# Attention: one value bank copied by ScalarE and one by VectorE, and the last step's output pieces in its first eight turns

## The chip, the core and the metric

The kernel runs on one core of a Trainium2 chip. The metric is the device time of one execution in microseconds; the time before is the median of three runs. One more execution was recorded by the hardware profiler, and all durations of single instructions come from it.

## What is computed

64 sequences of 32 tokens with 512 features go through four residual layers, all in fp32. The change touches the third, an attention over a paged cache followed by a small expert layer:

```python
q = einsum('bsd,ed->bse', x, Wq).reshape(B, S, HQ, D)      # 32 heads of 128
k, v = (einsum('bsd,ed->bse', x, W).reshape(B, S, HK, D) for W in (Wk, Wv))   # 8 heads
q, k = rope(rmsnorm(q)), rope(rmsnorm(k))
k_all = concat([k_cache[block_table], k], axis=1)          # 512 cached keys + 32 own
v_all = concat([v_cache[block_table], v], axis=1)
scores = where(valid, einsum('bqhd,bkhd->bhqk', q, repeat(k_all, 4)) * SCALE, -1e30)
o = einsum('bhqk,bkhd->bqhd', softmax(scores), repeat(v_all, 4))
return einsum('bse,de->bsd', o.reshape(B, S, HQ * D), Wo)
```

## The kernel before

Layers 0 and 1 come first and are not touched. In the attention (`attention`) the 2048 tokens are 16 tiles of 128 rows, four sequences each, and the heads are done in two halves of four key heads and sixteen query heads. That gives 32 *steps*, one for each half and tile, numbered 0 to 31. A step has 16 *turns*: four sequences (`b`) by four key heads (`g`). A turn `i` on TensorE is

- `turned(i)`: four transposes of the probabilities `pr` into a PSUM tile `prT_ps`, which ScalarE copies to `prT` (L790);
- `start(i + 2)`: the scores `sc` of the turn two ahead (L772), then on VectorE the masked minimum (L777), on ScalarE the exponential (L779), on VectorE the reciprocal and the scaling (L781, L784);
- `values`: the products of cached values `vt` and `prT` into `po` (L621).

Between these, work is placed by hand in `slots`: slot `2t` runs in turn `t` between the transposes and the scores, slot `2t + 1` between the scores and the values. The slots of a step hold the projections of the next step (pv, pk, pq), which the last step does not have; the eight pieces of the output projection of the previous step (`Output.product`, two products `py` each, from turn 9 on); the loads; and in the last step four small products `pw` that prepare the next layer (`tail.fold`, turns 10 to 13).

Two sequences make a *pair*. The values of a pair accumulate in two PSUM banks `pos[0]` and `pos[1]`, two heads each. At the end of a pair, in turns 7 and 15, `own_part` adds the products with the tokens' own values and copies both banks to `oT` (L820, VectorE). The next pair's first values product writes `pos[0]` again, so it waits for that copy. `oT` of a step is what the output pieces of the next step read: pieces 0 to 3 read the rows of `pos[0]`, pieces 4 to 7 those of `pos[1]`.

The keys of a sequence are 16 loads on SyncE's queue (`load_keys`, L98), with the page numbers read into SyncE's registers ahead of them (L93). There are two key buffers: the loads of sequence `b + 2` are placed in turn 1 of sequence `b`, and start when the last scores of `b` have been computed, in that same turn. They are needed two turns ahead of the sequence. GpSimd gathers the values (L643), SyncE also loads the earlier half's output `y_before` with piece 0 and stores the finished tile `y` (L755), which VectorE makes in L751. `y` and `y_before` have one buffer each.

After step 31 its own output pieces run in one go, and then the last layer (`tail.run`). The PE order is the program's order: every TensorE instruction of the attention is chained to the one before (`on_pe`).

Of the kernel before, what the change touches and what calls it, by code (L numbers as in the profile page):

```python
# [572 lines left out]
def attention(c, known, x_in, y_part, y_out, tail):  # L573
# [10 lines left out]
    tc, nc, a = c.tc, c.nc, c.a  # L584
    half = HD // 2
    n_c = L // P
    with ExitStack() as outer:
# [31 lines left out]
        def part(out, pairs, first, last):  # L619
            for i, (lhsT, rhs) in enumerate(pairs):  # L620
                c.on_pe(nc.tensor.matmul(out, lhsT, rhs, start=first and i == 0,  # L621
                                         stop=last and i == len(pairs) - 1))
# [56 lines left out]
        class Projection:  # L679
# [43 lines left out]
            def turned(self, what):  # L723
                r = self.r.pop(what)
                pt = transposes("tq", "qkT_ps", [r[:, m, :] for m in range(REP)])
                if what == "k":
                    nc.scalar.copy(self.kT, pt)
                else:
                    nc.scalar.copy(self.qT[:, what].rearrange("p j h s -> p h j s"),
                                   pt.rearrange("p h (j s) -> p h j s", j=SEQ))  # L730
# [62 lines left out]
        def own_turned(b):  # L793
            pt = transposes("tq", "own_prT_ps", [own_prs[b % 2]])
            own_prT = wk.tile([P, P], F32, name="own_prT", bufs=2)
            nc.scalar.copy(own_prT, pt[:, 0, :])
            return own_prT
# [3 lines left out]
        def values(b, g, prT):  # L801


            if b % 2 == 0 and g == 0:
                pos[:] = [ps.tile([P, 2, 2, P], F32, tag=f"po{n}", name="po") for n in range(2)]
            part(pos[g // 2][:, b % 2, g % 2, :], [(vts[b % 2][:, n, g * HD:(g + 1) * HD], prT[:, n, :])
                                                   for n in range(n_c)], b % 2 == 0 and g % 2 == 0, False)

        def own_part(b, own_prTs, oT):


            for u in range(2):
                for g in range(2):
                    for n in range(2):
                        q = slice(n * P // 2, (n + 1) * P // 2)
                        part(pos[n][:, u, g, :], [(own_vts[u][q, g, :], own_prTs[u][q, :])],
                             False, u == g == 1)
            at = (b - 1) % SEQ * S
            for n in range(2):
                nc.vector.tensor_copy(  # L820
                    oT[:, 2 * n * REP:2 * (n + 1) * REP, at:at + 2 * S]
                    .rearrange("p m (u s) -> p m u s", u=2),
                    pos[n].rearrange("p u g (h s) -> p (g h) u s", h=REP))
# [15 lines left out]
        steps = [(h, T) for h in range(HALVES) for T in range(NT)]  # L839
# [4 lines left out]
        def of(i):  # L844
            s, j, g = turns[i]
            h, T = steps[s]
            return s, h, SEQ * T + j, g
# [3 lines left out]
        def keys_of(i):  # L851
            if i < len(turns):
                s, h, b, _ = of(i)
                new_keys(h, b)
                own_keys(h, b, projections[s].kT)
                load_keys(h, b)

        def values_of(i):
            if i < len(turns):
                s, h, b, _ = of(i)  # L860
                load_values(h, b)

        def own_values_of(i):
            if i < len(turns):
                s, _, b, _ = of(i)
                own_values(b, projections[s].v)

        def start(i):
            if i < len(turns):
                s, h, b, g = of(i)  # L870
                scores(i, projections[s], h, b, g)
# [39 lines left out]
        for s, (h, T) in enumerate(steps):  # L911
            if s:
                oTs[s] = qp.tile([P, HQP, P], F32, name="oT")
            slots = [[] for _ in range(2 * per)]
            if s == 0:
                slots[0].append(partial(projections[0].turned, 2))
                slots[2].append(partial(projections[0].turned, 3))
                slots[2].append(partial(own_keys, 0, 1, projections[0].kT))
            if s + 1 < len(steps):
                p = projections[s + 1]  # L920
                for what, at in zip(("v", "k") + GROUPS,
                                    ((1, 2), (3, 4), (6, 7), (8, 10), (11, 13), (14, 16))):
                    for u in range(2):
                        slots[at[u]].append(partial(p.product, what, u))
                for what, at in zip(("k",) + GROUPS, (9, 12, 15, 17, 20)):
                    slots[at].append(partial(p.turned, what))
            else:
                slots[16].append(tail.scaled)
                for m, at in enumerate((20, 22, 24, 26)):
                    slots[at].append(partial(tail.fold, ps, m))  # L930
            if s + 2 < len(steps):
                slots[18].append(projections[s + 2].load)
                slots[24].append(projections[s + 2].tables)
                slots[28].append(projections[s + 2].x)
                if steps[s + 2][0] != h:

                    for what, at in zip(("v", "k") + GROUPS, (3, 5, 8, 11, 14, 17)):
                        slots[at].append(partial(weights, steps[s + 2][0], what))
            if s + 2 == len(steps):
                for at, f in zip((17, 20, 23, 26, 29), tail.weights(wp, wvk)):  # L940
                    slots[at].append(f)
            if s:
                out = Output(*steps[s - 1], oTs.pop(s - 1), ws)
                for u, at in enumerate((18, 19, 21, 23, 25, 27, 29, 31)):
                    slots[at].append(partial(out.product, u))
                if steps[s - 1][0] != h:
                    for u, at in enumerate((20, 24, 28, 31)):
                        slots[at].append(partial(output_weights, h, u))
                if s > 1:
                    slots[2].append(stores.pop(0))  # L950
                stores.append(out.store)
            for t in range(per):
                i = s * per + t
                _, _, b, g = of(i)
                prT = turned(i)
                if g == HKP - 1:
                    own_prTs = ([] if b % 2 == 0 else own_prTs) + [own_turned(b)]
                for f in slots[2 * t]:
                    f()
                start(i + 2)  # L960
                if g == 1:

                    keys_of(i - 1 + 2 * HKP)
                for f in slots[2 * t + 1]:
                    f()
                values(b, g, prT)
                if b % 2 and g == HKP - 1:
                    own_part(b, own_prTs, oTs[s])
                elif b % 2 == 0 and g in (0, 2) and i >= HKP:
                    own_values_of(i - g + g // 2 * HKP)  # L970
                if g == HKP - 1:
                    values_of(i - g + 2 * HKP)
# [222 lines left out]
def emit(tc, a, layers=(0, 1, 2)):  # L1195
    with ExitStack() as ctx:
        c = Common(ctx, tc, a)
        dram = ctx.enter_context(tc.tile_pool(name="scratch", bufs=1, space=DRAM))

        def scratch(name):  # L1200
            tiles = [dram.tile([P, D], F32, name=f"{name}_{t}") for t in range(NT)]
            return lambda t: tiles[t]

        def rows(name):
            return lambda t: a[name][t * P:(t + 1) * P, :]

        x = rows("x")
        for n in layers:
            out = rows("out") if n == layers[-1] else scratch(f"x{n}")
            if n == 0:  # L1210
                layer0(c, x, out)
            if n != 0 and n == next(m for m in layers if m):
                kp = ctx.enter_context(tc.tile_pool(name="known", bufs=1))
                last = Tail(c)
                last.numbers(kp)
                known = Known(c, kp)
            if n == 1:
                layer1(c, kp, x, out)
            elif n == 2:
                y_part, y = scratch("y_part"), scratch("y")  # L1220
                attention(c, known, x, y_part, y, last.between(x, y, out))
            x = out
# [86 lines left out]
```

## Time and profile before

| | us |
|---|---|
| median of three timed runs | 3705.31 (3702.78 to 3708.0) |
| the profiled execution | 3732.76 |
| its span, first to last instruction | 3730.8 |
| TensorE busy in the span | 3643.1 (98%) |
| VectorE, ScalarE, GpSimd busy | 1807.6, 1277.1, 1261.9 |

Times in the profile count from the start of the span. The attention's turns run from about 1100 to 3544 us, its last step from 3465.86, the last layer from 3560. PE is TensorE, PEld its weight loads, DVE VectorE, ACT ScalarE, POOL GpSimd, and SPq the queue of SyncE. In a row such as `3470.86 1.55 PE L621 MATMUL ... x8 [3.43 <-ACT prT L790]` the numbers are the start, the duration of the merged group, and in brackets how long the engine was idle before it and what ended that. In the chain the durations are issue times, without the overlapped tail of a product. Matmul counts are twice those of the source, [...]. PEclk is the granted share of the TensorE clock.

### The profile page before, as it was taken

How to read it: one execution, taken by the hardware profiler on the slowest of the kernel's cores; microseconds unless marked ns; L12 is line 12 of the kernel's file. 1: busy time of each engine (PE TensorE's matmuls, PEld its weight loads, DVE VectorE, ACT ScalarE, POOL GpSimd, SP SyncE). 2: the span in 40 equal slices, each digit the busy share in tenths (PEclk: the TensorE clock that was granted, in tenths of full speed). 3: DMA queues.
4: the chain of work that ended last, by engine and by line, in shares of the span. 5: the costliest groups of instructions: out<-in, count | busy, mean ns of one | idle time of the engine just before them, and what ended most of it. 6: DMA issues, size and time to landing. Idle time of an engine off the chain costs nothing.

```text
span 3730.8 us, 62064 instructions
## 1 busy us (share of the span) xinstructions
PE 3643.1 (98%) x18752; PEld 2526.2 (68%) x18752; DVE 1807.6 (48%) x4879; ACT 1277.1 (34%) x2950; POOL 1261.9 (34%) x1265
## 2 busy tenths in 40 slices
PE   6999999999999999999999999999999999999899
PEld 3444788888866777677667766677766776677655
DVE  5443222222236555565556555565556655565333
ACT  0111111211124444444444444444444444444311
POOL 0112100000035444544444444444445444444222
PEclk9999999999999999999999999999999999999999
DMA  5104211111044444334443356444444344434321
GB/s 195 34 24 162 99 43 60 43 49 36 32 145 129 123 119 124 115 116 119 121 118 114 117 177 188 153 125 122 122 127 122 118 123 123 123 117 143 119 71 60
DMA packets 408827, 407.68 MB, mean 109 GB/s; under 512 B 49232, under 2 KB 321616, under 8 KB 408496
## 3 DMA queue, kind: packets, MB, share of 16 engines
q1 hardware_dynamic: 361776, 251.65, 22.1%
q0 software_dynamic: 44416, 147.88, 12.8%
q10 hardware_dynamic: 2304, 4.20, 0.3%
q8 instruction: 152, 2.49, 0.3%
q14 instruction: 179, 1.47, 0.1%
HBM read 382.57 MB, written 20.97 MB: 108 GB/s over the span
## 4 chain that ended last, share of the span: by engine, by line
PE 93%; SPq 2%; issue 1%; DVE 1%; another core or an unknown queue 1%; DMA 1%; DVEq 1%; ACT 1%; POOL 0%; ACTq 0%; POOLq 0%
PE po L621 14%; PE sc L772 12%; PE pq L621 11%; PE py L621 11%; PE gate_up L292 10%; PE prT_ps L616 6%; PE pz L292 5%; PE po L1079 3%; PE pk L621 3%; PE ph L122 3%; PE pv L621 3%; PE pd L228 2%; PE po L292 2%; PE qkT_ps L616 2%; PE py L183 1%
## 5 line engine op out<-in xcount | busy, mean ns | idle before, releaser
L643 POOL DMA_INDIRECT vt<-in_v_rows,v_rows x512 | 500.7, 978 | 805.6 <-PE po L621 693.2
L621 PEld LDWEIGHTS po<-prT,vt 128*128 128x128 f32 x4096 | 530.6, 192 | 212.2 <-issue 185.1
L777 DVE CUSTOM_DVE_ANT_0 pr<-sc,mask 128x544 f32<-128x544 f32 x512 | 368.7, 720 | 477.7 <-PE sc L772 394.0
L772 PE MATMUL sc<-kt,qT 128*128 128x288 f32 (+1 forms) x2048 | 557.6, 395 | 12.2 <-DMA kt<-in_kT 8.0
L621 PE MATMUL po<-prT,vt 128*128 128x128 f32 x4096 | 545.3, 276 | 22.1 <-ACT prT L790 18.5
L779 ACT ACTIVATE pr<-pr,low 128x544 f32<-128x544 f32 x512 | 383.6, 749 | 486.7 <-DVE low L777 484.4
L772 PEld LDWEIGHTS sc<-kt,qT 128*128 128x128 f32 x2048 | 369.8, 191 | 189.9 <-issue 83.9
L621 PE MATMUL py<-wo,oT 128*128 128x512 f32 x1024 | 480.5, 593 | 0.8 <-DVE oT L820 0.8
L621 PE MATMUL pq<-wq,xT 128*128 128x512 f32 x1024 | 480.8, 593 | 0.0
L790 ACT COPY prT<-prT_ps 128x512 f32<-128x512 f32 x512 | 298.6, 583 | 441.2 <-PE prT_ps L616 279.6
L784 DVE TENSOR_SCALAR pr<-pr,low 128x512 f32<-128x512 f32 x512 | 324.1, 633 | 16.8
L616 PE MATMUL prT_ps<-ident,pr 128*128 128x128 f32 x2048 | 312.2, 275 | 0.0
L621 PEld LDWEIGHTS py<-wo,oT 128*128 128x128 f32 x1024 | 192.3, 190 | 137.8 <-issue 125.8
L621 PEld LDWEIGHTS pq<-wq,xT 128*128 128x128 f32 x1024 | 182.5, 190 | 130.0 <-issue 125.2
L781 DVE RECIPROCAL low<-low 128x1 f32<-128x1 f32 x512 | 83.4, 163 | 360.0 <-ACT pr L779 321.3
L616 PEld LDWEIGHTS prT_ps<-ident,pr 128*128 128x128 f32 x2048 | 239.0, 142 | 7.6
L126 POOL TENSOR_TENSOR rs<-rs,minus_half 128x4 f32<-128x4 f32 x160 | 166.2, 1039 | 168.3 <-DVE rs L659 166.2
L675 POOL TENSOR_TENSOR rot<-rot,swapped 128x512 f32<-128x512 f32 x160 | 202.6, 1266 | 1.0
L782 ACT ACTIVATE own_pr<-pr,low 128x32 f32<-128x32 f32 x512 | 164.3, 321 | 107.6 <-DVE low L781 104.8
L676 POOL TENSOR_TENSOR rot<-rot,rs 128x512 f32<-128x512 f32 x160 | 181.0, 1132 | 8.0
L376 DVE TENSOR_TENSOR sg<-sg,gate_up 128x256 f32<-128x256 f32 (+1 forms) x88 | 37.0, 420 | 278.4 <-ACT sg L375 278.4
L292 PE MATMUL gate_up<-xT,gate1T 128*128 128x256 f32 (+1 forms) x704 | 168.2, 382 | 0.0
(207 smaller groups left out, 4594.6 us busy)
## 6 DMA issues: line engine op xcount, KB each, us to landing
kt<-in_kT SPq DMA_DIRECT2D x2048, 64.0 KB
xt<-x SPq DMA_DIRECT2D x48, 256.0 KB
wq<-in_WqT SPq DMA_DIRECT2D x12, 1024.0 KB
A<-in_A SPq DMA_DIRECT2D x64, 152.0 KB
sets<-in_cond0T SPq DMA_DIRECT2D x4, 2048.0 KB
vt<-in_v_rows,v_rows POOLq DMA_INDIRECT x512, 3.7
wo<-in_WoT SPq DMA_DIRECT2D x8, 1024.0 KB
y<-y SPq DMA_DIRECT2D x32, 256.0 KB
```

The lines of the kernel that those rows point to most:

```text
L126: self.nc.gpsimd.tensor_tensor(t, t, self.minus_half[:, :n], ALU.pow)
L292: c.on_pe(nc.tensor.matmul(out, lhsT, rhs, start=start, stop=stop))
L616: c.on_pe(nc.tensor.transpose(pt[:, m, :], piece, c.ident))
L621: c.on_pe(nc.tensor.matmul(out, lhsT, rhs, start=first and i == 0, stop=last and i == len(pairs) - 1))
L643: nc.gpsimd.indirect_dma_start(out=vts[b % 2][:, n, :], out_offset=None, in_=a["v_rows"], in_offset=bass.IndirectOffsetOnAxis(ap=rows[h][: ...
L675: nc.gpsimd.tensor_tensor(r, r, tmp, ALU.add)
L676: last = nc.gpsimd.tensor_tensor(r, r, rs.unsqueeze(2).to_broadcast([P, REP, HD]), ALU.mult)
L772: c.on_pe(nc.tensor.matmul(sc[:, lo + n * PSIZE:lo + m * PSIZE].rearrange("p (n k) -> p n k", k=PSIZE), q, kt[:, n:m, g, :], start=True, s ...
L777: nc.vector.tensor_tensor_reduce(pr[:, :NK], sc[:, lo:lo + NK], masks[h, b], -SCALE, 3.0e38, ALU.add, ALU.min, low[:, 0:1])
L779: nc.scalar.activation(pr[:, :NK], pr[:, :NK], AF.Exp, bias=low[:, 0:1], scale=-1.0, accum_out=low[:, 1:2])
L784: nc.vector.tensor_scalar(pr[:, :L], pr[:, :L], low[:, 2:3], None, ALU.mult)
L790: nc.scalar.copy(prT, pt)
```

## The change

Of the two copies at the end of a pair, that of `pos[0]` is issued on ScalarE and that of `pos[1]` on VectorE. In the last step the eight output pieces of step 30 are placed in slots 1, 3, 5, ... 15, one in each of turns 0 to 7 between scores and values, and no longer in slots 18 to 31. All other steps keep their slots.

```diff
             at = (b - 1) % SEQ * S
-            for n in range(2):
-                nc.vector.tensor_copy(
+            for n, copy in enumerate((nc.scalar.copy, nc.vector.tensor_copy)):
+                copy(
                     oT[:, 2 * n * REP:2 * (n + 1) * REP, at:at + 2 * S]
                     .rearrange("p m (u s) -> p m u s", u=2),
                     pos[n].rearrange("p u g (h s) -> p (g h) u s", h=REP))
...
             if s:
                 out = Output(*steps[s - 1], oTs.pop(s - 1), ws)
-                for u, at in enumerate((18, 19, 21, 23, 25, 27, 29, 31)):
+
+                ats = (18, 19, 21, 23, 25, 27, 29, 31) if s + 1 < len(steps) else range(1, 16, 2)
+                for u, at in enumerate(ats):
                     slots[at].append(partial(out.product, u))
```

## The prediction

> **What bounds the kernel now.** I read the page first: which engine carries the chain of work that ended last.
>
> ```profile
> PE 93%; SPq 2%; issue 1%; DVE 1%; another core or an unknown queue 1%; DMA 1%; DVEq 1%; ACT 1%; POOL 0%; ACTq 0%; POOLq 0%
> ```
>
> TensorE is the bound. VectorE (48% busy) and ScalarE (34%) count only where TensorE waits for them, so moving a copy from one to the other is worth nothing by itself. Next, the stretches view: the last two rows are the two halves (eight turns each) of the last step, the row before them is the second half of step 30, still full.
>
> ```profile
> core 0: us, PE busy (x) PEld busy (x) DVE busy (x) ACT busy (x) POOL busy (x), PEclk, DMA share, GB/s
> ...
> 3428.18:3465.86 37.68, 37.68 (x215) 27.29 (x214) 19.95 (x59) 17.33 (x41) 13.83 (x15) 1.00 0.57 184
> 3465.86:3507.64 41.78, 28.79 (x165) 24.23 (x164) 19.56 (x58) 14.71 (x37) 10.60 (x11) 0.85 0.52 159
> 3507.64:3544.34 36.70, 36.65 (x171) 23.96 (x170) 10.39 (x26) 10.47 (x25) 6.61 (x6) 0.98 0.15 47
> ```
>
> The first half of the last step has the least TensorE work of all (no projections, no output pieces), takes the longest, and lowers the granted clock to 0.85. The second half, which has the eight output pieces and four folds, is full. The waits of TensorE in that first half, and of ScalarE:
>
> ```profile
> PE po L621 <- ACT prT L790: 9.2, 3, 3.5
> PE sc L772 <- DMA kt<-in_kT: 3.8, 2, 2.6
> ```
>
> ```profile
> ACT prT L790 <- remote: 12.0, 3, 5.8
> ```
>
> So 13.0 us idle: 9.2 for the transposed probabilities `prT`, whose ScalarE copy itself waits for something the profile cannot name, and 3.8 for keys. The keys come at SyncE's pace:
>
> ```profile
> 3462.09 10.51 SPq L98 DMA_DIRECT2D kt<-in_kT  x16
> ...
> 3481.03 26.47 SPq L98 DMA_DIRECT2D kt<-in_kT  x32
> ```
>
> One sequence costs SyncE 16 loads at 0.525 us (undisturbed) plus 6.8 us to read its page numbers: 15.2 us. Four bare turns of TensorE take 9. With projections in them they take 19, and SyncE keeps up.
>
> **The change part by part.** Issue times per turn come from the chain, here in step 31's predecessor: output piece 1.72, scores 0.92, values 0.89, transposes 0.44; a fold is 1.72 like a piece, the own-value products of a pair 1.10, an own-probability transpose 0.11.
>
> ```profile
> 3435.16 1.72 PE py L621 x4
> 3436.88 0.92 PE sc L772 x4
> 3437.79 1.72 PE py L621 x4
> 3439.51 0.89 PE po L621 x8
> 3440.40 0.44 PE prT_ps L616 x4
> ```
>
> *Last step before*, in work: 16 x 0.44 + 14 x 0.92 + 16 x 0.89 + 8 x 1.72 + 4 x 1.72 + 2 x 1.10 + 4 x 0.11 = 57.4 us. It takes 78.5 (3465.86 to 3544.34). The lost 21 us: 13.0 idle, most of the rest three stretches at half clock (3471.5 to 3474.9, 3492.0 to 3498.8, 3505.6 to 3509.0).
>
> *Last step after*, first half: 8 x (0.44 + 0.92 + 1.72 + 0.89) + 0.22 + 1.10 = 33.1. The pieces sit between scores and values, where each covers the `prT` copy (0.58 us) and gives SyncE time. Keys of sequence 62 are needed at turn 6, which TensorE now reaches at 3465.9 + 6 x 3.97 + 0.55 = 3490.3; SyncE, which stood still with the other engines for 5 us before its last load at 3490.9, would without that have issued it at about 3486 and landed it 1.9 later. Keys of 63 (15.2 us on, landed at 3503) are needed in turn 10, at 3505.7. Both just fit; a miss of 2 us is inside my range. Second half: 8 x 0.44 + 6 x 0.92 + 8 x 0.89 + 4 x 1.72 + 0.22 + 1.10 = 24.4, plus what is late next: turns 14 and 15 have no scores, so with the pieces gone nothing covers their `prT` copies, 0.7 + 0.9 us; turn 8, 0.1. Together 26.1; the step 59.2 us.
>
> *What moves with the pieces.* Their `y_before` load moves on SyncE's queue from behind the page numbers of 62 to ahead of them. It waits for the addition of step 29, which ends at 3464.7, and is issued after 3473: no wait, 0.33 us in the same batch. The store of step 30 stays behind the loop; the addition on VectorE (0.69 us) moves from turn 15 to turn 7, beside TensorE work. GpSimd's queue is untouched: its value gathers wait for the same `po` products, now later by the pieces. Piece 0 in turn 0 reads the bank ScalarE has just copied: ready 0.75 us after the own products, read at 1.36. With both copies on VectorE behind its own-value copies it would be 1.8: the two edits belong together.
>
> *The copy, 64 times.* VectorE loses 64 x 0.69 = 44 us off the path: nothing. ScalarE gains 64 copies. Nearest row, the same 128x512 strided eviction:
>
> ```profile
> L729 ACT COPY qT<-qkT_ps x128: 564/586/593, 1091.7 to 3441.4; 128x512 f32<-128x512 f32 x128
> ```
>
> 0.586 us, below VectorE's 0.690. [...] Taking the VectorE duration instead would add 0.1 per copy; I take the row. What queues behind: the copy waits for the pair's own products, and directly behind it stands the next turn's `prT`, on which TensorE's values wait. A boundary in the loop:
>
> ```profile
> 3391.57 1.29 DVE L820 COPY oT<-po 128x512 f32<-128x512 f32 x2
> ...
> 3391.91 0.58 ACT L790 COPY prT<-prT_ps 128x512 f32<-128x512 f32 x1 [2.87 <-PE prT_ps L616]
> ...
> 3393.60 1.05 PE L621 MATMUL po<-prT,vt 128*128 128x128 f32 x8
> ```
>
> `prT` is done at 3392.49, values start at 3393.60: 1.1 us of slack, made by the projection piece in front. The copy can start when the own products end, 0.5 us before the transposes do, so at most 0.1 us of it delays `prT`: cost 0. Uncovered it would be 0.59 at each of 62 inner boundaries, 36 us; that is the upper bound. Below zero it can hardly go: no boundary there waits for VectorE.
>
> *The end.*
>
> ```profile
> 3545.06 14.00 PE L621 MATMUL py<-wo,oT 128*128 128x512 f32 x32 [0.78 <-DVE oT L820]
> ```
>
> The last step's own pieces wait 0.78 for the first bank; ScalarE's shorter copy saves 0.1.
>
> *Which of the stalls are in the timed runs?* By the trace alone the step goes from 78.5 to 59.2: 19.3 us less, 16 if one stall stays in turn 8. But during the three `prT` stalls several engines stand still at once: SyncE's register moves take up to 0.71 us between 3467.6 and 3470.1 where 0.03 is usual, and again at 3483.5 to 3486.1; TensorE's records say that the transposes were done 3.7 us before their semaphore came. [...] the timed kernel has less to gain: 78.5 - 9.2 = 69.3 before, so 69.3 - 59.2 = 10.1, less 0.3 for the keys' close timing, about 9.8 us. The profiled execution took 3732.76 us (span 3730.8, 2.0 around it) against a median of 3705.31, so 27 us of profiling are somewhere[...]. So against the profiled execution's own 3732.76 the sum is 16 to 19 less, 3714 to 3717; against the median I take 3705.31 - 9.8 = 3695.5.
>
> **The rivals.**
>
> *A, likeliest (0.54):* as above; 3691 to 3700.
>
> *B, the stalls are real (0.20):* timed runs have them and the pieces absorb them. Gain 16 to 19: about 3688. For it: the clock really halves after them. Against it: SyncE stalls too, and it has no part in `prT`.
>
> *C, nothing to win (0.19):* SyncE runs faster when not profiled, keys are never late, the clock never halves. Then before is 57.4 plus 1 to 2 of exposed copies and after the same: 0 to 5 us, about 3702. Against it: [...] turn 6 missed its keys by 3.8 us although the stalls had held TensorE (5.7 us) as long as SyncE (5).
>
> *D, slower (0.07):* ScalarE's copy delays `prT` at the boundaries. In about half of the step boundaries of the profile `prT` starts late and values already wait 0.2 us, so the cover there is thin. It decides from (9.8 + 7.4) / 62 = 0.28 us lost per boundary; at the full 0.59 the loss is 36 and the time 3705.3 + 36 - 9.8 = 3731. At 0.4, 3720. Against it: in those boundaries ScalarE is idle for over a microsecond between the own products and the transposes.
>
> That the change does not do what it says is excluded by the instruction order: TensorE's is the same up to the last step, one oT copy stands per pair on each engine, and all eight pieces precede turn 8's transposes.
>
> **How the numbers follow.** A change of 0.2% (7.4 us) is about what a measurement of this kernel can tell from none. Faster by more: three quarters of A (0.41), all of B (0.20), a little of C (0.02): 0.63. Slower by more: most of D, 0.05. Within: 0.32. The range 3687 to 3703 leaves out the far part of B (0.05), the small end of C (0.08) and D (0.06).
>
> **What would show it.** In the profile after: the first half of the last step near 33 to 37 us with TensorE full and the clock near 1; no key wait in turns 6 and 10; the second half near 26, with two new waits on `prT` in turns 14 and 15; `oT` by ScalarE at about 0.59; the same stretches before 3465.86 unchanged within 1 us. I am wrong if steps 0 to 30 change length (D), if the last step shrinks as forecast but the timed gain is under 5 us (C) or over 14 (B), or if keys make TensorE wait at turn 6 as before.

## The result, and the profile after

The changed kernel takes 3694.8 us (median of 11 runs, 3690.4 to 3697.93) against 3705.31 for the kernel before beside it (11 runs, 3700.33 to 3711.01). The ratio is 0.9973, with a 95% interval of 0.9964 to 0.9982: 10.5 us less. The forecast was 3695.5. The profiled execution after took 3697.93 us with a span of 3695.9 and is the slowest of the 11 runs. The profiled execution before (3732.76) lay outside its own runs; why is asked below.

The chain of work of the profile after, shares by engine. TensorE is still the bound, and nothing has taken its place:

```profile
PE 93%; SPq 3%; DMA 1%; issue 1%; DVE 1%; ACT 0%; POOL 0%; DVEq 0%; ACTq 0%; POOLq 0%
```

The stretches view of the profile after. The cuts are the second half of step 30 and the two halves of step 31, at the ends of the pairs' own products:

```profile
core 0: us, PE busy (x) PEld busy (x) DVE busy (x) ACT busy (x) POOL busy (x), PEclk, DMA share, GB/s
3411.70:3449.43 37.73, 37.73 (x216) 27.37 (x214) 18.74 (x58) 18.05 (x42) 14.04 (x15) 1.00 0.58 189
3449.43:3482.50 33.07, 32.88 (x174) 23.56 (x174) 14.96 (x45) 14.91 (x35) 7.58 (x8) 1.00 0.48 145
3482.50:3510.74 28.24, 26.31 (x166) 19.70 (x162) 13.67 (x37) 11.37 (x29) 8.38 (x10) 1.00 0.43 132
```

The forecast's cut of the profile of before was another one: it took 3507.64 for the middle of the step, but the pair's own products end at 3500.7 there, so its "first half" of 41.78 us holds nine turns and its second seven. Cut after eight turns, the first half of before is

```profile
3465.86:3500.70 34.84, 25.34 (x148) 21.28 (x146) 14.65 (x45) 12.97 (x33) 7.79 (x9) 0.85 0.45 141
```

and the second, with one of the three `prT` waits in its first turn, 43.6 us. The first half, which had TensorE busy for 25.3 of 34.8 us at a clock of 0.85, is now full at 1.00, with the output pieces in it. The step is 61.3 us long (from the end of step 30's own products to the end of its own), against 78.4 in the profile of before. TensorE's waits between 3440 and 3516, and SyncE's DMA issues over the same time:

```profile
PE po L621 <- ACT prT L790: 1.6, 3, 0.8
PE py L621 <- ACT oT L820: 0.7, 1, 0.7
PE sc L772 <- DMA kt<-in_kT: 0.2, 1, 0.2
```

```profile
3453.21 0.37 SPq L85 DMA_DIRECT2D y_before<-y_part  x1
3453.63 0.43 SPq L755 DMA_DIRECT2D y<-y  x1
3462.63 25.47 SPq L98 DMA_DIRECT2D kt<-in_kT  x32
```

SyncE needs as long for the 32 loads of sequences 62 and 63 as before (25.5 against 26.5 us), but TensorE now has work until they land: 0.2 us of waiting for keys in place of 3.8. `y_before` goes out ahead of them and holds nothing up. The price is the bare turns 14 and 15, where nothing stands between the transposes and the values (TensorE's rows of the profile after):

```profile
3506.23 1.16 PE L621 MATMUL po<-prT,vt 128*128 128x128 f32 x8 [0.84 <-ACT prT L790]
...
3508.55 1.16 PE L621 MATMUL po<-prT,vt 128*128 128x128 f32 x8 [0.62 <-ACT prT L790]
```

The two copies of a pair, from the profile's view of line 820:

```profile
L820 ACT COPY oT<-po x64: 564/584/587, 1144.0 to 3510.8; 128x512 f32<-128x512 f32 x64
L820 DVE COPY oT<-po x64: 691/692/693, 1145.7 to 3510.9; 128x512 f32<-128x512 f32 x64
```

**What the profile of before had that its timed runs had not.** The 34.9 us between the two spans are far more than the change. From pair 2 to pair 60 (start of the own products), where only the copy is different, the profile of before took 2218.84 us and that of after 2204.69. So the forecast's "unchanged within 1 us" ahead of the last step is wrong by 14 us. The profile after is not clean there either: a second profile of the same kernel, *after_again* below, has 2200.14, and the 4.5 us between them lie at the change from the first half of the heads to the second (near 2302 us), where TensorE waits 3.1 us for keys and then has a granted clock of 0.50 from 2302.2 to 2305.6.

The three groups of experiments ran on three different chips, and runs of one kernel differ between them: in the first group of experiments below the kernel before has a median of 3723.39 us, in the second and third 3705.93 and 3705.56. Each comparison is inside one group.

### The profile page after: what moved, and what is told of

The parts are those of the page before. It is cut to its first block, busy times and chain, and to the rows that moved or that the text cites. A ratio compares the mean times of both kernels' runs of the same rounds, so it can differ in the third digit from the quotient of the medians.

```text
span 3695.9 us, 62123 instructions
## 1 busy us (share of the span) xinstructions
PE 3630.8 (98%) x18752; PEld 2525.1 (68%) x18752; DVE 1803.3 (49%) x4815; ACT 1316.3 (36%) x3014; POOL 1259.4 (34%) x1265
## 4 chain that ended last, share of the span: by engine, by line
PE 93%; SPq 3%; DMA 1%; issue 1%; DVE 1%; ACT 0%; POOL 0%; DVEq 0%; ACTq 0%; POOLq 0%
PE po L621 14%; PE sc L772 12%; PE pq L621 12%; PE py L621 11%; PE gate_up L292 10%; PE prT_ps L616 6%; PE pz L292 5%; PE po L1081 3%; PE pv L621 3%; PE pk L621 3%; PE ph L122 3%; PE pd L228 2%; PE po L292 2%; PE qkT_ps L616 2%; PE py L183 1%; SPq L93 1%
## 5 line engine op out<-in xcount | busy, mean ns | idle before, releaser
L784 DVE TENSOR_SCALAR pr<-pr,low 128x512 f32<-128x512 f32 x512 | 364.5, 712 | 16.8
```

The source lines that it names most:

```text
L784: nc.vector.tensor_scalar(pr[:, :L], pr[:, :L], low[:, 2:3], None, ALU.mult)
```

## The experiments

In the expectations of the first four runs, P is the theory of the prediction, that the long `prT` waits belong to recording a profile (an assumption of the author, which no row of the trace shows), and R is its rival, that they are real and come from the two copies on VectorE.

### First group: each edit alone, and the folds later (before: 3723.39 us)

*before_again* is the kernel before, unchanged.

> The kernel before, unchanged, profiled a second time. Theory P (the stalls at which several engines stand still belong to recording the profile): a new profile shows them again at pair boundaries, 5 us or more of idle TensorE before values that wait for prT, and its execution is again 15 us or more above the timed median near 3705. Theory Q (the first profile caught one disturbed execution): the boundaries are clean, the profiled time is within 5 us of the median, and the last step takes 67 to 71 us instead of 78.5, with the key wait of turn 6 at 4 us or more. Theory R (two VectorE copies in a row at a boundary cause the stalls): stalls again, and at the same boundaries, also in the timed runs.

Measured: 3723.81 us, ratio 0.9998 (0.9990 to 1.0006); the profiled execution took 3722.86, in the middle of its runs. The waits are there again. Of its timeline, turn 0 of the last step:

```profile
3464.93 0.59 ACT L790 COPY prT<-prT_ps 128x512 f32<-128x512 f32 x1 [5.69 <-remote]
3464.99 0.72 DVE L777 CUSTOM_DVE_ANT_0 pr<-sc,mask 128x544 f32<-128x544 f32 x1 [0.99 <-remote]
3465.56 1.35 PEld L621 LDWEIGHTS po<-prT,vt 128*128 128x128 f32 x6 [3.73 <-ACT prT L790]
```

ScalarE and VectorE start again within 0.06 us of each other, each after a wait that no row explains, and TensorE's values wait 3.3 us for `prT`. The profiled time is the time of the timed runs, so that only the profiled execution has these waits does not hold on this chip. (Every timed run on record comes with a span and a granted clock, so some recording may be on in all of them; what speaks most clearly against P is *before_again2* below, recorded in the same way and free of the waits.)

*copy_only* has the copy edit and the old slots.

```diff
-            for n in range(2):
-                nc.vector.tensor_copy(
+            for n, copy in enumerate((nc.scalar.copy, nc.vector.tensor_copy)):
+                copy(
```

> Only the first edit: ScalarE copies one bank, VectorE the other; the output pieces of the last step stay in turns 9 to 15. My sum: within 2 us of before (3703 to 3706), since TensorE waits for neither copy at a full boundary; the gain all comes from the slots. Theory R: 4 us or more faster, as 14 us of boundary time are missing between the two profiles in steps 0 to 30. Rival D of the prediction: slower.

Measured: 3720.24 us, ratio 0.9989 (0.9981 to 0.9998), 3.2 us less. The wait of turn 0 is there with ScalarE's copy too (TensorE's rows):

```profile
3461.28 0.94 PE L621 MATMUL po<-prT,vt 128*128 128x128 f32 x6 [3.36 <-ACT prT L790]
```

So the pair of VectorE copies does not make it, and R falls in that form.

*slots_only* has the new slots and both copies on VectorE.

```diff
-                for u, at in enumerate((18, 19, 21, 23, 25, 27, 29, 31)):
+
+                ats = (18, 19, 21, 23, 25, 27, 29, 31) if s + 1 < len(steps) else range(1, 16, 2)
+                for u, at in enumerate(ats):
```

> Only the second edit: the output pieces of step 30 in turns 0 to 7 of the last step; both banks copied by VectorE. My sum: 9 to 10 us faster than before (3695 to 3697), half a microsecond behind the full change, because piece 0 and the first values of turns 0 and 8 wait for VectorE's copies behind its own-value copies, and the last 16 products wait 0.1 longer. Theory R: 4 to 7 us faster only.

Measured: 3715.61 us, ratio 0.9977 (0.9968 to 0.9985), 7.8 us less. The pieces do not absorb the long wait. It turns up in turn 8, the first turn with no piece over the copy (TensorE's row):

```profile
3502.28 0.94 PE L621 MATMUL po<-prT,vt 128*128 128x128 f32 x6 [3.38 <-ACT prT L790]
```

*folds_late* is the changed kernel with its four folds spread over the second half.

```diff
-                for m, at in enumerate((20, 22, 24, 26)):
+                for m, at in enumerate((20, 24, 29, 31)):
```

> The full change, and two of the four folds moved from turns 11 and 13 to slots 29 and 31, so that they stand between transposes and values in turns 14 and 15 (the others in turns 10 and 12). If TensorE's two new waits there, 0.84 and 0.62 us, are simply uncovered copies, they vanish: 1.2 to 1.5 us faster than the full change, about 3693. If the bare turns 11 and 13 then wait for their probabilities (a score is ready for transposing 2.45 us after its last product, a bare turn takes 2.25), 0.2 to 0.5 of it is given back in each.

Measured: 3710.94 us, ratio 0.9965 (0.9952 to 0.9978). The waits of turns 14 and 15 are gone, a long one of 3.35 us stays in turn 8. In all five profiles that have long `prT` waits (before and these four) values also wait 1.6 to 1.8 us for `prT` at the same four places, near 1175, 2240, 2320 and 2400 us, whatever the edit. So the waits are tied to places of the program, and not scattered by chance.

### Second group: what paces the last step (before: 3705.93 us)

*after_again* is the changed kernel.

> The changed kernel beside before on the chip of this call. If the gain of the changed kernel belongs to the two edits and not to the chip: ratio near 0.997 (0.996 to 0.998), about 8 to 12 us less than before, whether or not the long prT waits with several engines standing still turn up in its profile. If the first chip made the difference (no such waits in the profile there): less than 5 us here.

Measured: 3695.29 us, ratio 0.9969 (0.9957 to 0.9981): 10.6 us less. Its profile (span 3690.6) has no long `prT` wait. Its two halves of step 31:

```profile
3444.94:3478.11 33.17, 33.17 (x181) 24.02 (x179) 15.46 (x47) 14.90 (x35) 7.80 (x9) 1.00 0.48 147
3478.11:3505.46 27.35, 25.55 (x156) 19.37 (x154) 13.16 (x35) 11.38 (x29) 7.59 (x8) 1.00 0.42 131
```

*folds_late2* repeats folds_late beside it.

> The changed kernel with its four folds in slots 20, 24, 29, 31 in place of 20, 22, 24, 26, so that the last two cover the prT copies of turns 14 and 15. If the two waits there (0.84 and 0.62 in the profile after) cost what they show, 1 to 1.5 us less than the changed kernel beside it; if TensorE only loses them elsewhere (the folds' own VectorE work, the end of the step), no difference over 0.5 us.

Measured: 3693.47 us, ratio 0.9962 (0.9949 to 0.9976). In the profile the second half is 25.63 us long (27.35 with the folds where they were), slightly more saved than expected:

```profile
3485.53:3511.16 25.63, 25.30 (x156) 19.09 (x154) 13.08 (x35) 11.45 (x29) 9.08 (x9) 1.00 0.46 141
```

Of the 1.8 us between the two medians the intervals cannot tell whether they are real. It is the lowest ratio of the versions that do the whole work.

*both_scalar* gives ScalarE both copies.

```diff
-            for n, copy in enumerate((nc.scalar.copy, nc.vector.tensor_copy)):
+            for n, copy in enumerate((nc.scalar.copy, nc.scalar.copy)):
```

> The changed kernel with both banks copied by ScalarE, none by VectorE: the nearest way to the rival in which ScalarE's copies delay prT. Two copies of 0.586 in a row end about 1.0 to 1.2 us later than one, against 1.1 us of slack that prT had before and 0.1 of it used by the first copy. If the slack is as read from the profile: about 0 to 0.2 us per pair boundary, 0 to 12 us more than the changed kernel, most likely 3. If boundaries have less slack than the one shown: 0.3 to 0.6 each, 19 to 36 us more. If copying on ScalarE itself is what saves (the copies no longer wait behind VectorE's own work): less than the changed kernel by up to 3 us.

Measured: 3693.99 us, ratio 0.9965 (0.9952 to 0.9979), no more than the changed kernel. ScalarE's rows at the pair end before step 31:

```profile
3445.11 1.07 ACT L820 COPY oT<-po 128x512 f32<-128x512 f32 x2 [1.53 <-PE po L621]
3446.07 0.60 ACT L790 COPY prT<-prT_ps 128x512 f32<-128x512 f32 x1
```

After nearly every pair `prT` starts 2.15 to 2.25 us behind the first own product, 0.4 later than in the changed kernel (1.79). Yet pair 2 to pair 60 takes 2200.45 us against 2200.14. The projection piece covers this delay too.

*keys_one* is the kernel before with one load for each of the last two sequences' keys; the pages are other ones, which is the part of the computation that changes.

```diff
+            if h and b >= 62:
+                c.last_load = nc.sync.dma_start(kts[h, b][:, :NPP, :],
+                                                a["kT"][0:NPP, h].rearrange("a d f -> d a f")).ins
+                return
             pages = c.numbers(a["pages"][0:1, b * NPP:(b + 1) * NPP], PAGES)
```

> The kernel before with the keys of the last two sequences (62 and 63 of the second half) loaded by one DMA of the first 16 pages each, in place of 16 loads at page numbers read into SyncE's registers: the only part that is changed, so these two sequences attend to other pages. If SyncE's pace for the keys is what TensorE waits for in the last step: the waits sc <- DMA kt (2.0 to 4.7 us in the profiles of before) go, and 3 to 6 us with the half-clock stretches behind them. If the prT waits come first and the keys would only be the next in line: key waits go but the time stays within 1.5 us. If SyncE's dense register moves also bring the prT waits of the last step: those go too (6 to 8 us more).

Measured: 3695.2 us, ratio 0.9970 (0.9959 to 0.9981): 10.7 us less than before, the whole gain of the change, with neither of its edits. It was expected to give 3 to 6. The two halves of step 31:

```profile
3445.87:3468.12 22.25, 20.82 (x149) 17.33 (x147) 14.63 (x45) 12.57 (x33) 7.80 (x9) 1.00 0.86 250
3468.12:3507.66 39.54, 38.44 (x188) 25.45 (x186) 15.23 (x39) 12.10 (x29) 9.41 (x9) 1.00 0.22 68
```

Here the first half stays short (22.25 us) and the second has the pieces: 61.8 us together, where the changed kernel has 33.17 + 27.35 = 60.5. The DMA share of 0.86 at 250 GB/s, against 0.51 at 155 in the first half of *before_again2* below, tells that the transfers themselves can run faster than they did; what TensorE waited for was SyncE's issuing, page-number reads and loads together, which this run does not separate. Both sequences also read the same 16 pages here, which lie together; what that alone is worth was not measured.

### Third group: before on such a chip, and whether the remedies add (before: 3705.56 us)

*before_again2* is the kernel before, unchanged.

> The kernel before, unchanged, profiled once more. If the long prT waits belong to the chip that a run falls on: beside timed runs near 3706 its profile shows none of them, the profiled time lies among the timed ones, and the last step takes 70 to 72 us (60.5 of the changed kernel on such a chip and the 10.6 that it gains there) with key waits of 2 to 5 us and a half-clock stretch behind them as the whole loss. Beside timed runs near 3723 it shows them again. If they belong to recording a profile: prT waits in the profile and timed runs near 3706.

Measured: 3704.96 us, ratio 0.9998 (0.9989 to 1.0006), profiled execution 3702.86, among the timed ones. The same two halves, and TensorE's rows of turn 6:

```profile
3444.59:3474.86 30.27, 23.20 (x149) 18.87 (x147) 14.64 (x45) 12.68 (x33) 7.81 (x9) 0.89 0.51 155
3474.86:3514.39 39.53, 38.44 (x188) 25.45 (x186) 15.23 (x39) 12.11 (x29) 9.40 (x9) 1.00 0.29 92
```

```profile
3466.25 1.30 PE L772 MATMUL sc<-kt,qT 128*128 128x288 f32 x2 [4.25 <-DMA kt<-in_kT]
3468.49 1.19 PE L772 MATMUL sc<-kt,qT 128*128 128x256 f32 x2 [0.94 <-DMA kt<-in_kT]
3469.47 1.91 PE L621 MATMUL po<-prT,vt 128*128 128x128 f32 x8
```

No long `prT` wait is left. The last step is 69.8 us, and its loss in the first half is keys: 6.4 us of waiting, 5.2 of it in turn 6 and 1.2 in turn 2, and products at about half clock behind it, 1.91 us for the values that take 1.05 elsewhere (the granted clock is 0.50 from 3464.6 to 3471.4). SyncE sent the last load of sequence 62 at 3466.53, and the wait ends 1.96 us later. Against keys_one the first half is 8.0 us longer.

*copy_only2* and *slots_only2* are the two edits alone, once more.

> Only the copy edit: the first bank by ScalarE, the output pieces where they were. If the copy is off the path at every boundary: within 1.5 us of before. If the 3 to 4 us of the first measurement are real: 2 to 5 us less.

> Only the pieces moved, both copies by VectorE. If the moved pieces give all of the gain: 9 to 12 us less than before. If the two edits belong together, because piece 0 in turn 0 reads the bank that a VectorE copy delivers late (2.2 to 2.9 us after the own products begin, against 1.2 to 1.8): 1 to 2 us of that missing.

Measured: copies alone 3702.03 us, ratio 0.9991 (0.9983 to 1.0000); slots alone 3695.54, ratio 0.9971 (0.9959 to 0.9984), 10.0 us less. The slots give all that can be told apart in time. For the copies, 3.5 us less after 3.2 in the first group is twice the same sign, but each interval reaches to 0 or close to it, and 3.5 and 10.0 together would be more than the 10.6 of the whole change. The profile of copy_only2 has a smaller effect, in the last step alone; its pairs 2 to 60 are 4.3 us longer than those of before_again2, mostly by the wait for keys at the change of the heads' halves (2.3 us there, 0.9 in before_again2, 0.4 in after_again, 3.1 in the profile after), which comes and goes with and without the edits. In before_again2 turn 8's values stood still for 1.09 us until VectorE, behind its own-value copies, had emptied the first bank (a reading from the times: the first of its two copies ends at about 3477.4):

```profile
3476.73 1.29 DVE L820 COPY oT<-po 128x512 f32<-128x512 f32 x2
3477.49 0.97 PEld L621 LDWEIGHTS po<-prT,vt 128*128 128x128 f32 x8 [1.47 <-issue]
3477.52 1.13 PE L621 MATMUL po<-prT,vt 128*128 128x128 f32 x8 [1.09 <-issue]
```

With ScalarE's copy 0.12 of it is left, and the second half is 38.60 us in place of 39.53. With the slots alone, piece 0 waits for VectorE's copy (TensorE's row of slots_only2), and in the changed kernel it does not:

```profile
3446.97 1.99 PE L621 MATMUL py<-wo,oT 128*128 128x512 f32 x4 [0.27 <-DVE oT L820]
```

The last step is 62.56 us with the slots alone and 60.52 with both (*after_again*); 0.69 of the difference is a wait for keys, which the copy does not explain.

*keys_one_after* is the changed kernel with the edit of keys_one (other pages for the last two sequences).

> The changed kernel with the keys of sequences 62 and 63 loaded by one DMA of the first 16 pages each (these two sequences attend to other pages). If key pacing is what the moved pieces cure, the two remedies do not add: within 1.5 us of the changed kernel. If the moved pieces gain by something else (TensorE fuller, clock), about 10 us less than the changed kernel, so 20 less than before.

Measured: 3693.27 us, ratio 0.9963 (0.9949 to 0.9977). The last step is 60.52 us, the same as without the edit. The two remedies do not add: both end the same wait.

## Why the prediction came out right, and where it did not

**The bound and the cause held.** SyncE's pace for the keys is what lengthened the last step; keys_one and keys_one_after show it by timed runs alone, so rival C (0 to 5 us to win) falls. The time of before without the `prT` waits was put at 69.3 us; it is 69.80 in before_again2. That this is so close is in part luck: the sum took away the 9.2 us of `prT` waits and left all else as it was, but without them the keys make TensorE wait 6.4 us and not 3.8, turn 8 waits 1.1 us for VectorE's copy, and 6.8 us at a granted clock of 0.50 are left of 13.6 us. The last step after was put at 59.2; it is 60.52 and 61.31. So the step gains 9.3 us by clean profiles (10.1 forecast), and the timed gain is 10.5 and 10.6 (9.8 forecast).

**First half: 33.1 forecast, 33.17 and 33.59 measured.** "Both just fit" holds: TensorE waited for the keys of 62 in turn 6 by 0.19 us in the profile after, not at all in after_again, 0.34 in folds_late2 and 0.69 in slots_only2; for those of 63 in turn 10 by 1.14 in both_scalar, not at all in after_again. The margin is as thin as it was put.

**Second half: 26.1 forecast, 27.35 and 27.72 measured.** The waits in turns 14 and 15 are as expected in sum (0.84 and 0.62 against 0.7 and 0.9). What was mis-sized is above all turns 8 and 9, put at 4.5 us of work and 0.1 of wait: from 3483.01 to the transposes of turn 10 at 3488.45 they take 5.44 us. The rest is turn 14, 2.43 us where work and wait were put at 2.03, and in this profile alone turn 10, 4.34 in place of 3.97. In turn 9 the chain of the profile after comes to the copy of `prT` only by way of VectorE:

```profile
3484.08 0.27 DVE own_vt L650
3484.35 0.01 issue
3484.36 0.69 DVE oT L820
3485.05 0.01 issue
3485.07 0.22 DVE own_vt L650
3485.29 0.03 issue
3485.32 0.72 DVE pr L777
```

The minimum that the next turns need stands behind the own-value copies and the second bank's copy, and ScalarE has the exponential that waits for it ahead of turn 9's `prT`.

**The copy.** Its size held (0.584 measured, 0.586 forecast), and so did "cost 0 at the boundaries": pair 2 to pair 60 takes 2200.51 us in before_again2 and 2200.14 in after_again, and `prT` starts 1.79 us behind the first own product in both. The slack was read too small: the boundary that the forecast shows is one of those where `prT` starts late (2.53 us behind, as it does by 2.2 or more in 53 of 63 boundaries of that profile). In before_again2 it is 1.85 us at most boundaries, not 1.1, so the cover that rival D called thin is thick when the long waits are absent. Rival D was further off than its 0.07 said: both_scalar delays `prT` by 0.4 us per boundary, more than the 0.28 of lost time from which D decides, and loses nothing, because the delay never gets past the piece in front. But "no boundary there waits for VectorE" was read from a boundary that has a projection piece; turn 8 of the last step has none and waited 1.09 us. "The two edits belong together" holds for that wait and for piece 0 (0.27 us); in the time the slots alone give 10.0 of 10.6 us. VectorE is not relieved of the 44 us either: its busy time is 1811.3 us in before_again2 and 1802.0 in after_again, because its scaling of `pr` (L784) takes 712 ns in the mean in the profile after in place of 626. Its median stays at 487 ns; why more of them take long stays open. Of the two copies ScalarE's is the shorter one, 0.584 against 0.692 us.

**Which stalls are in the timed runs: the number was right, the reason wrong.** The step that failed is the one that took the 9.2 us of `prT` waits out of the sum: that they belong to profiling was the author's assumption, and no trace shows it. On the chip of the first group the long waits are in executions whose profiled time is an ordinary timed one (TensorE's values wait 12.4 us for `prT` in before_again, 13.4 in copy_only, 13.1 in slots_only); on the chips of the other groups they are missing in profiles recorded in the same way (0.2 us in before_again2 and in copy_only2). They go with the chip or the hour, not with recording alone and not with one of the kernels. That the timed runs of the result seem free of them (their median before, 3705.31, is that of the chips without them) was luck: the reason given did not foresee it. That the first profile was taken where such waits occur, and its timed runs were not, fits the 29.9 us between its span (3730.8) and that of before_again2 (3700.9): 18.3 in pairs 2 to 60, 8.6 in the last step. The forecast of 3714 to 3717 for the profile after and "unchanged within 1 us" failed for the same reason. Rival B fails too: where the stalls are in timed runs, the gains are 7.8 us with the slots alone and 12.4 in folds_late (the changed kernel itself was not run there), not 16 to 19; one long wait moves on to turn 8. What makes engines stand still there, at the same places of the program each time, was not found and stays open.

## What to carry to other kernels

When the last pass of a pipelined loop lacks the work that the others have, compare what is left with the pace of the slowest queue feeding it: here 9 us of products per sequence against 15 us of register reads and loads. Moving work from a full half into the starved one, or making the feed cheaper by one wide load, are two cures of the same wait, and only one pays (the wide load of keys_one read pages that lie together). Before a stall of a profile goes into the sum, compare the profiled execution's time with the timed runs: where it lies outside them, as 3732.76 us does outside 3700.33 to 3711.01 here, the profile holds something that they do not, and a second profile is worth more than an assumption about it.

## What was not expected of the hardware

The kernel before took 3723.39 us on the chip of the first group (42 runs, 3715.72 to 3737.61) and 3705.93 and 3705.56 on the others, 18 us or 0.5% apart, with waits for `prT` of up to 3.4 us that no row explains. One load of 16 pages in place of 16 loads with page numbers saved 10.7 us for two sequences, more than the 5.7 us of waiting for keys that it removes (6.4 before, 0.7 left): the products right behind the wait had run at a granted clock of 0.50 (1.91 us for the values in place of 1.05), and the first half of the step was 8.0 us shorter in the profile. Most of the other 2.7 us may be that the profiled execution of before_again2 lay 2.1 us below the median of its runs.
